# FFN columns on partitions between up and down, with block transposes around the quantization, and all clips on GpSimd from the fifth unit on

## The chip, the cores and the metric

The kernel runs on one core of a Trainium2 chip. Five of the core's parts matter here: TensorE (PE in the profile, with its weight loads as PEld), VectorE (DVE), ScalarE (ACT), GpSimd (POOL), and the queue of SyncE (SP), which issues nearly all transfers. The metric is the device time of one execution in microseconds. Before the change it is 3705.63 us, the median of three runs from 3700.53 to 3706.57.

## The reference

One transformer layer over x of 8 sequences by 1024 tokens by 512, all in float32: a layer norm, latent attention (16 heads, 32 content and 16 rotary dimensions a head, scores clipped to +-80, causal softmax), a residual, a second layer norm, a feed-forward network whose linear layers quantize both operands to FP4 in blocks of 16 along the contracted dimension, and a residual.

```python
def fp4_quant_dequant(x):                       # BLOCK = 16, along the last dim
    xb = x.reshape(shape[:-1] + (shape[-1] // BLOCK, BLOCK))
    scale = jnp.maximum(jnp.max(jnp.abs(xb), axis=-1, keepdims=True) / 6.0, 1e-12)
    xn = xb / scale
    idx = jnp.searchsorted(_MID, jnp.abs(xn))
    return (_GRID[idx] * jnp.sign(xn) * scale).reshape(shape)

gate = fp4_linear(x, w_gate)                    # w_gate, w_up: 1408 x 512
y = fp4_linear(x, w_up)
h = jax.nn.silu(gate) * y
return fp4_linear(h, w_down)                    # w_down: 512 x 1408
```

So the 1408 columns of h are quantized in blocks of 16 neighbours before the last product contracts over them.

## The kernel before

The 8192 tokens are cut into 16 units of 512 (two per sequence), each of 4 tiles of 128 tokens; the FFN has 64 tiles. The orders of PE, DVE and ACT are written out by the program: it runs its Python loops once and keeps, in `Clock`, an estimate of when each of the three engines will be free. DVE work that isn't urgent waits in two queues, `soon` (sums of the softmax, norms of x) and `later` (FFN norms and quantization). `on_dve` places an instruction that has a due time and first fills the estimated gap ahead of it from the queues; `need(key)` places all that is queued up to a key, just before PE uses that result. GpSimd's and SyncE's instructions stand in the order in which the program makes them.

*Attention* (`attention`, `score_step`). For each group of four heads, and each block of 128 keys, PE makes scores into one PSUM tile, ACT takes exponentials in two halves, each half is clipped (the first by DVE, L531, the second by GpSimd, L534), GpSimd masks both halves of the diagonal blocks (L538), DVE adds the weights up (L560; from the fifth unit on always, `FIRST = 4`), and PE multiplies them with the values one step later. The clip of the first half goes through `on_dve`, so it is also a point where queued DVE work is placed.

*Fillers.* Between the steps PE gets pieces of other work from a list, in proportion to cost: the next unit's projections, in the first four units the quantization and transposition of the weights (`weight_pieces`), and from the fifth unit on the FFN (`ffn_pieces`). After the last step of attention the rest of the FFN runs alone: some four and a half tiles.

*FFN per tile of 128 tokens.* Tokens lie on the partitions. `fetch` loads y from the memory where `out_proj` left it, `begin` queues its norm and its quantization, `turned` has PE transpose y in four blocks of 128x128 (`turn`, L184) and ACT copy them out. `gate` and `up` multiply with the transposed y as the stationary operand and the weights moving, in three pieces of 512, 512 and 384 columns (`FCH`); ACT copies gate out (L126), takes silu of all 1408 columns at once (L730), and DVE multiplies up into it (L742). `quantize` treats the 1408 columns as one: the maxima of its 88 blocks (L197), six small instructions for the scales (L202 to L207), then per piece a scaling (L224), two instructions for the step (L232, L235), an addition and a subtraction that round to it (L238), and the scaling back (L220). Then PE transposes h in 11 blocks (`hidden_turned`, three groups of 4, 4 and 3), ACT copies these out as hT (L186), and `down` contracts over 11 blocks, 512 columns wide. Between up and down of a tile lie down of the tile before and gate of the tile after.

Every fp32 matmul is two passes of PE in the profile, each with a weight load; the count of a group is that of passes.

*Norms.* `normed` has DVE take mean and variance (L302 to L304), GpSimd raise the variance to the power -0.5 (L305), and DVE apply both (L308). DVE's next instruction after L304 is mostly L308 itself.

Of the kernel before, what the change touches and what calls it, by code (L numbers as in the profile page):

```python
# [42 lines left out]
def tile_mla_then_fp4_ffn(  # L43
# [22 lines left out]
    p4 = ctx.enter_context(tc.tile_pool(name="p4", bufs=4))  # L66
    small = ctx.enter_context(tc.tile_pool(name="small", bufs=2))
# [121 lines left out]
    def quantize(q, width, key):  # L189
        nb = width // BLK  # L190
        q3 = q.rearrange("p (b k) -> p b k", k=BLK)
        got = {}

        def amax():
            got["sc"] = sc = p1.tile([P, 88], F32, tag="sc", name="sc")[:, :nb]
            got["rs"] = rs = p1.tile([P, 88], F32, tag="rs", name="rs")[:, :nb]
            nc.vector.tensor_reduce(rs, q3, AX.X, ALU.max, apply_absolute_value=True)  # L197
# [11 lines left out]
        slack(0.06 + 0.0011 * width, amax, key)  # L209
        slack(1.1 + 0.008 * nb, scales, key)  # L210
        for o in range(0, width, 512):
            step = min(512, width - o)
            part, bl = q[:, o : o + step], slice(o // BLK, (o + step) // BLK)
# [31 lines left out]
            slack(pass_cost, lambda f=times: f("sc"), key)  # L245


    def weight_pieces():
# [10 lines left out]
        def load(i):  # L259

            if i % 3 < 2:
                raw = p2.tile([P, FF], F32, tag="h", name="wraw")
            else:
                raw = p1.tile([P, NFC, P], F32, tag="hT", name="wraw_hT")
                raw = raw.rearrange("p n k -> p (n k)")
            raws[i], at = raw, 0
            for src, _ in chunks[i]:
                nc.sync.dma_start(out=raw[:, at : at + src.shape[1]], in_=src)
                at += src.shape[1]
            quantize(raw[:, :at], at, ("w", i))  # L270

        def piece(i, at, dst, off, n):
            if i == 0 and at == 0:
                for k in range(3):
                    load(k)
            clk.need(("w", i))
            turn(raws[i][:, at : at + n * P], dst[:, off : off + n], n)
            if at + n * P == sum(src.shape[1] for src, _ in chunks[i]):
                raws.pop(i)
                if i + 3 < len(chunks):  # L280
                    load(i + 3)

        pieces = []
        for i, parts in enumerate(chunks):
            at = 0
            for src, dst in parts:
                for off, width in FCH if src.shape[1] == FF else [(0, D)]:
                    n = width // P
                    pieces.append((i, at, dst, off // P if src.shape[1] == FF else 0, n))
                    at += width  # L290
# [33 lines left out]
    def project_pieces(u):  # L324
# [31 lines left out]
        def rotation(g):  # L356
# [15 lines left out]
            krp = p1.tile([P, 256], F32, tag="krp", name="krp")  # L372
# [103 lines left out]
    def score_step(u, hq, j, qc, qr, acc, aT):  # L476
# [48 lines left out]
        for k, (half, ready) in enumerate(zip(halves, done)):  # L525
            part = pT[:, half, :cols]
            if k == 0:
# [100 lines left out]
    def attention(u):  # L628
# [6 lines left out]
        total, gone = sum(c for c, _ in fillers), 0.0  # L635
        aTs = []
        for hq in range(NQ):
# [5 lines left out]
            for j in range(nj):  # L643
# [7 lines left out]
                while fillers and (gone + fillers[0][0] / 2) * whole < total * spent:  # L651
                    c, run = fillers.popleft()
# [11 lines left out]
    mids, outs = {}, {}  # L664
# [5 lines left out]
    def out_proj(u, t, aTs):  # L670
# [19 lines left out]
        mids[u, t] = mid  # L690
        if t == NT - 1:
            del live["wo"]


    tiles = [(u, t) for u in range(2 * B) for t in range(NT)]
    ys, hs, ends = {}, {}, {}
# [5 lines left out]
    def begin(n):  # L702
        begin_norms([(ys[n], ("y", n))])
        quantize(ys[n], D, ("y", n))

    def hidden(n, w, off, width):
        pg = bank("pg")[:, :width]
        for i in range(NDC):
            mm(
                pg,  # L710
                lhsT=ys[n][:, i, :],
                rhs=w[:, i, off : off + width],
                start=(i == 0),
                stop=(i == NDC - 1),
            )
        return pg

    def turned(n):
        clk.need(("y", n))
# [217 lines left out]
```

## Time and profile before

| | us |
|---|---|
| median of three runs | 3705.63 |
| the profiled execution | 3706.02 |
| its span, first to last instruction | 3704.3 |
| PE busy | 3611.4 |
| DVE busy | 2702.0 |
| ACT busy | 1279.7 |
| POOL busy | 660.9 |

Busy times are sums over the span; a wait is the idle time of an engine ahead of an instruction, put down to what ended it. Matmuls overlap in the pipeline, so a matmul's duration is longer than the distance to the next; what a row of matmuls costs is read from their starts. "xN" is a number of instructions.

### The profile page before, as it was taken

To read this page: it belongs to the slowest core of one execution; us is meant where nothing else is said; L and a number is where in the kernel's file an instruction comes from. 1 tells how busy PE (TensorE), PEld (TensorE's weight loads), DVE (VectorE), ACT (ScalarE), POOL (GpSimd) and SP (SyncE) were. 2 spreads that over 40 slices of the span, in tenths; PEclk is the share of its full clock that TensorE was granted. 3 is DMA by queue.
4 is the path that set the end of the run, shared out by engine and by line. 5 is a ranking of instruction groups with operands and counts; after the bars stand their busy time and mean duration, and the time that the engine had idled before them with its cause. 6 is when DMAs were issued, how large, how long until landed. Compare 5 with 4: busy or idle time off the path is not lost.

```text
span 3704.3 us, 45379 instructions
## 1 busy us (share of the span) xinstructions
PE 3611.4 (97%) x18052; PEld 1632.5 (44%) x18052; DVE 2702.0 (73%) x4775; ACT 1279.7 (35%) x1722; POOL 660.9 (18%) x838
## 2 busy tenths in 40 slices
PE   7898989999999999999999999999999999999999
PEld 3333334444444444444444444444444444444444
DVE  5866846777776787776777676878667787768875
ACT  3343443333323333333333233333233333333311
POOL 2223221111111111111111111111111111111200
PEclk9999999999999999999999999999999999999999
DMA  3101101010010100020100101000110001010010
GB/s 84 58 30 53 63 17 43 24 57 24 18 57 18 54 18 23 18 63 23 43 23 18 57 24 49 21 20 27 54 43 23 23 18 57 18 46 18 15 60 15
DMA packets 75884, 131.20 MB, mean 35 GB/s; under 512 B 13720, under 2 KB 14744, under 8 KB 75672
## 3 DMA queue, kind: packets, MB, share of 16 engines
q1 hardware_dynamic: 73824, 127.17, 10.9%
q8 instruction: 142, 2.33, 0.3%
q10 hardware_dynamic: 1848, 1.13, 0.1%
q14 instruction: 70, 0.57, 0.1%
HBM read 94.72 MB, written 33.55 MB: 35 GB/s over the span
## 4 chain that ended last, share of the span: by engine, by line
PE 83%; DVE 1%; ACT 1%; DMA 1%; POOL 0%; issue 0%; SPq 0%; ACTq 0%; POOLq 0%
PE pg L113 32%; PE pd L113 17%; PE sc_ps L113 11%; PE num L113 6%; PE po L113 5%; PE pt L184 3%; PE pp L113 2%; PE den L113 1%; PE pqr L113 1%; PE pk L113 1%; PE pv L113 1%; PE pq L113 1%; ACT pT L516 1%; DMA wo<-in_w_o_dram 0%; PE pf L113 0%
## 5 line engine op out<-in xcount | busy, mean ns | idle before, releaser
L516 ACT ACTIVATE pT<-sc_ps 128x1024 f32<-128x1024 f32 (+1 forms) x640 | 566.0, 936 | 1004.9 <-PE sc_ps L113 779.2
L113 PE MATMUL pg<-wu_T,yT 128*128 128x512 f32 (+1 forms) x1536 | 637.2, 562 | 6.9 <-ACT kT L126 5.1
L113 PE MATMUL pd<-wd_T,hT 128*128 128x512 f32 x1408 | 640.6, 596 | 0.0
L113 PE MATMUL pg<-wg_T,yT 128*128 128x512 f32 (+1 forms) x1536 | 632.7, 563 | 1.5 <-ACT yT L186 1.5
L534 POOL TENSOR_SCALAR pT<-pT 128x1024 f32<-128x1024 f32 (+1 forms) x320 | 336.4, 1051 | 1063.2 <-ACT pT L516 742.7
L538 POOL TENSOR_SCALAR_AFFINE_SELECT pT<-pT 128x256 f32<-128x256 f32 (+1 forms) x384 | 239.3, 623 | 1539.9 <-DVE pT L531 1228.7
L560 DVE TENSOR_TENSOR pT<-pT 128x1024 f32<-128x1024 f32 (+3 forms) x528 | 464.6, 904 | 8.0 <-POOL pT L538 4.6
L531 DVE TENSOR_SCALAR pT<-pT 128x1024 f32<-128x1024 f32 (+1 forms) x320 | 213.7, 668 | 342.8 <-ACT pT L516 341.8
L113 PEld LDWEIGHTS pg<-wg_T,yT 128*128 128x128 f32 x1536 | 287.7, 191 | 329.4 <-issue 259.5
L113 PEld LDWEIGHTS pg<-wu_T,yT 128*128 128x128 f32 x1536 | 281.7, 191 | 295.1 <-issue 231.2
L113 PEld LDWEIGHTS pd<-wd_T,hT 128*128 128x128 f32 x1408 | 255.4, 191 | 280.7 <-issue 270.5
L113 PE MATMUL sc_ps<-qc,kT 32*128 32x512 f32 (+3 forms) x3072 | 340.2, 527 | 4.3 <-ACT pT L516 4.2
L113 PE MATMUL num<-pT,v 128*32 128x512 f32 (+3 forms) x3072 | 321.8, 498 | 10.7 <-POOL pT L538 6.3
L742 DVE TENSOR_TENSOR h<-pg,h 128x512 f32<-128x512 f32 (+1 forms) x192 | 123.7, 644 | 279.2 <-PE pg L113 267.1
L113 PE MATMUL sc_ps<-qr,kr 32*128 32x512 f32 (+3 forms) x3072 | 306.5, 483 | 4.3 <-DVE qr L452 4.3
L126 ACT COPY h<-pg 128x512 f32<-128x512 f32 (+1 forms) x192 | 105.5, 550 | 544.4 <-PE pg L113 544.4
L238 DVE TENSOR_TENSOR h<-h,m 128x512 f32<-128x512 f32 (+1 forms) x384 | 261.1, 680 | 10.5
L113 PE MATMUL po<-wo,aT 128*128 128x512 f32 x512 | 224.7, 597 | 11.6 <-DMA wo<-in_w_o_dram 10.3
L186 ACT COPY hT<-pt 128x512 f32<-128x512 f32 (+1 forms) x192 | 105.4, 550 | 302.6 <-PE pt L184 302.0
L113 PEld LDWEIGHTS sc_ps<-qc,kT 32*128 32x128 f32 x3072 | 114.8, 184 | 200.7 <-issue 157.4
L113 PEld LDWEIGHTS sc_ps<-qr,kr 32*128 32x128 f32 x3072 | 145.6, 186 | 108.6 <-issue 82.4
L113 PEld LDWEIGHTS num<-pT,v 128*32 128x32 f32 x3072 | 67.0, 108 | 217.5 <-issue 142.4
(99 smaller groups left out, 3615.4 us busy)
## 6 DMA issues: line engine op xcount, KB each, us to landing
xo<-in_x_dram SPq DMA_DIRECT2D x64, 256.0 KB, 2.7
wo<-in_w_o_dram SPq DMA_DIRECT2D x16, 1024.0 KB, 5.4
mid<-xo SPq DMA_DIRECT2D x64, 256.0 KB, 2.3
y<-mid SPq DMA_DIRECT2D x64, 256.0 KB, 2.6
xr<-mid SPq DMA_DIRECT2D x64, 256.0 KB, 2.6
out_dram<-xr SPq DMA_DIRECT2D x64, 256.0 KB, 2.0
xl<-in_x_dram SPq DMA_DIRECT2D x62, 256.0 KB, 2.7
wraw<-in_w_gate_dram SPq DMA_DIRECT2D x8, 256.0 KB, 2.7
```

What stands on the lines that cost most here:

```text
L113: nc.tensor.matmul(dst, **kw)
L126: on_act(0.1 + 0.0009 * src.free_size(), lambda: nc.scalar.copy(dst, src))
L184: nc.tensor.transpose(pt[:, i, :], src[:, i * P : (i + 1) * P], ident)
L186: on_act(0.56, lambda: nc.scalar.copy(dst, pt[:, 0:n, :]))
L238: nc.vector.tensor_tensor(part, part, got["m"], op)
L516: lambda: nc.scalar.activation(part, sc[:, 2 * k : 2 * k + 2, :cols], AF.Exp, scale=SM_SCALE),
L531: lambda: nc.vector.tensor_scalar(part, part, E_HI, E_LO, ALU.min, ALU.max),
L534: nc.gpsimd.tensor_scalar(part, part, E_HI, E_LO, ALU.min, ALU.max)
L538: nc.gpsimd.affine_select(out=diag, in_=diag, pattern=[[0, 2], [0, len(segs)], [1, P]], compare_op=ALU.is_ge, fill=0.0, base=0, channel_mu ...
L560: lambda a=whole, b=part: nc.vector.tensor_tensor(a, a, b, ALU.add),
L742: lambda: nc.vector.tensor_tensor(h, pg, h, ALU.mult),
```

## The change

The FFN works on pairs of tiles (256 tokens). `turned` still transposes y per tile, into two halves of 256 tokens (`yTs`). `hidden` has the weights stationary and y moving: each of the 11 blocks of 128 columns of gate and up comes out with the columns on the partitions and 256 tokens along the free axis, two blocks to a PSUM tile, so six pieces of gate and six of up a pair. `down` takes h as it lies, as the stationary operand; `hidden_turned`, the tile hT and its copies are gone. Since 16 neighbouring columns now lie on 16 partitions, `quantize` with `turned=True` has DVE transpose each part in place in blocks of 32x32 before the maxima and again after the scaling back. h is quantized in three groups a pair (two pieces each; in the last pair the last two pieces are groups of their own), each queued as soon as its last up is through, and silu is taken after every second piece of gate. The order of a pair is gate 0, 1, up 0, 1, both downs of the pair before, gate 2, 3, up 2, 3, gate 4, 5, up 4, 5, with the loads and norms of the next pair between. The parts come from a pool `ring` of nine tiles of 512 columns, which the weights' loads use too.

From the fifth unit on (`u >= FIRST`) GpSimd clips both halves of a step. The rotary product of the keys (`krp`) is written into the place of its result. Pieces of the FFN carry their tile, and attention doesn't take a piece whose tile has not gone through `out_proj`.

```diff
+    ring = ctx.enter_context(tc.tile_pool(name="ring", bufs=9))
...
-    def quantize(q, width, key):
-        nb = width // BLK
-        q3 = q.rearrange("p (b k) -> p b k", k=BLK)
+    def quantize(parts, key, turned=False):
+        ends, at = [], 0
+        for part in parts:
+            ends.append((at, at + part.shape[1] // BLK))
+            at = ends[-1][1]
+        nb = at
...
+        def turn_blocks(part):
+            slack(
+                0.06 + 0.0013 * part.shape[1], lambda: nc.vector.transpose(part, part), key
+            )
...
-        slack(0.06 + 0.0011 * width, amax, key)
+        for k, part in enumerate(parts):
+            if turned:
+                turn_blocks(part)
+            slack(0.06 + 0.0012 * part.shape[1], lambda k=k: amax(k), key)
         slack(1.1 + 0.008 * nb, scales, key)
...
             slack(pass_cost, lambda f=times: f("sc"), key)
+            if turned:
+                turn_blocks(part)
...
-            if i % 3 < 2:
-                raw = p2.tile([P, FF], F32, tag="h", name="wraw")
...
+                for off in range(0, src.shape[1], 512):
+                    width = min(512, src.shape[1] - off)
+                    raw = ring.tile([P, 512], F32, tag="h", name="wraw")[:, :width]
+                    nc.sync.dma_start(out=raw, in_=src[:, off : off + width])
...
-            krp = p1.tile([P, 256], F32, tag="krp", name="krp")
+            krp = proj[u][2][:, g * 256 : (g + 1) * 256]
...
-            if k == 0:
+            if k == 0 and u < FIRST:
                 on_dve(
...
+                    if len(fillers[0]) > 2 and tiles[fillers[0][2]] not in projected:
+                        break
...
-        quantize(ys[n], D, ("y", n))
-    def hidden(n, w, off, width):
-        pg = bank("pg")[:, :width]
+        quantize([ys[n]], ("y", n))
+    def turned(n):
+        m, t = divmod(n, 2)
+        clk.need(("y", n))
+        if t == 0:
+            yTs[m] = [ring.tile([P, 2, 256], F32, tag="h", name="yT") for _ in range(2)]
+        pt = bank("pt").rearrange("p (n k) -> p n k", k=P)
         for i in range(NDC):
-            mm(
-                pg,
-                lhsT=ys[n][:, i, :],
-                rhs=w[:, i, off : off + width],
-                start=(i == 0),
-                stop=(i == NDC - 1),
-            )
+            nc.tensor.transpose(pt[:, i, :], ys[n][:, i * P : (i + 1) * P], ident)
+            clk.pe += 0.11
+        ys.pop(n)
+        for i in range(2):
+            to = yTs[m][i][:, :, t * P : (t + 1) * P]
+            on_act(0.38, lambda: nc.scalar.copy(to, pt[:, 2 * i : 2 * i + 2, :]))
+    def hidden(m, w, k):
+        n = min(2, NFC - 2 * k)
+        pg = bank("pg").rearrange("p (n k) -> p n k", k=256)[:, :n]
+        for c in range(n):
+            f0 = (2 * k + c) * P
+            for i in range(NDC):
+                mm(
+                    pg[:, c, :],
+                    lhsT=w[:, i, f0 : f0 + P],
+                    rhs=yTs[m][i // 2][:, i % 2, :],
+                    start=(c == 0 and i == 0),
+                    stop=(c == n - 1 and i == NDC - 1),
+                    skip_group_check=True,
+                )
         return pg
...
+        if k % 2 == 1:
+            def silu(hk=hs[m][k - 1 :]):
+                for h in hk:
+                    on_act(0.2 + 0.0009 * h.free_size(), lambda: nc.scalar.activation(h, h, AF.Silu))
+                clk.act += 2.6
+            silus.append(silu)
...
+        for group in ((0, 1), (2, 3), (4,), (5,)) if m == pairs - 1 else ((0, 1), (2, 3), (4, 5)):
+            if k == group[-1]:
+                quantize([flat(hs[m][j]) for j in group], ("h", m, k // 2), True)
...
-    def hidden_turned(n, k):
...
-        turn(hs[n][:, off : off + width], hTs[n][:, f0 : f0 + c, :], c)
...
     def down(n):
-        hT = hTs[n]
+        m, t = divmod(n, 2)
+        if t == 0:
+            fetch_x1(n + 1)
         pd = bank("pd")
-        for i in range(NFC):
-            mm(pd, lhsT=hT[:, i, :], rhs=wd_T[:, i, :], start=(i == 0), stop=(i == NFC - 1))
...
+        for c in range(NFC):
+            if t == 0 and c % 4 == 0:
+                clk.need(("h", m, c // 4))
+            mm(
+                pd,
+                lhsT=hs[m][c // 2][:, c % 2, t * P : (t + 1) * P],
+                rhs=wd_T[:, c, :],
+                start=(c == 0),
+                stop=(c == NFC - 1),
+            )
...
+            yield from run(gate, 0)
+            if m > 0:
+                yield 0.0, n, lambda m=m: fetch_x1(2 * m - 2)
+            if m < last:
+                yield 0.0, n + 2, lambda n=n: fetch(n + 1)
+                yield 0.0, n + 2, lambda n=n: fetch(n + 2)
+            yield from run(gate, 1)
+            if m < last:
+                yield 0.0, n + 2, lambda n=n: begin(n + 1)
+            yield from run(up, 0, 1)
+            if m > 0:
+                yield 9.6, n, lambda m=m: down(2 * m - 2)
+                yield 9.6, n, lambda m=m: down(2 * m - 1)
+            if m < last:
+                yield 0.0, n + 2, lambda n=n: begin(n + 2)
+            yield from run(gate, 2, 3)
+            yield from run(up, 2, 3)
+            yield from run(gate, 4, 5)
+            if m < last:
+                yield 0.5, n + 2, lambda n=n: turned(n + 1)
+            yield from run(up, 4)
+            if m < last:
+                yield 0.5, n + 2, lambda n=n: turned(n + 2)
+            yield from run(up, 5)
```

## The prediction

> **What bounds the kernel now.** I read the page first (shares, the span in 40 slices), then busy time by stretch, then who waits for whom, then groups by form, then stretches of the timeline for the spacing of instructions, which the groups' means don't give.
>
> ```profile
> PE 3611.4 (97%) x18052; PEld 1632.5 (44%) x18052; DVE 2702.0 (73%) x4775; ACT 1279.7 (35%) x1722; POOL 660.9 (18%) x838
> ...
> PE   7898989999999999999999999999999999999999
> ...
> DVE  5866846777776787776777676878667787768875
> ...
> PEclk9999999999999999999999999999999999999999
> ```
>
> PE is full from the seventh slice to the end, at the full clock. DVE, the next engine, is at six to eight tenths.
>
> ```profile
> 900.00:1200.00 300.00, 297.37 (x1427) 136.70 (x1426) 218.75 (x389) 104.08 (x141) 50.01 (x68) 1.00 0.10 32
> ...
> 3300.00:3600.00 300.00, 297.80 (x1302) 133.03 (x1301) 240.34 (x415) 94.45 (x119) 44.36 (x50) 1.00 0.09 29
> ```
>
> Columns: length, then busy PE, PEld, DVE, ACT, POOL, clock, DMA. Over 600 to 3650 us the stretches leave PE idle for 17.5 us in all; 69 us lie in the first 600 us and 6 in the last 54. So in the FFN part an instruction taken from PE is worth its spacing, as long as no other engine comes late.
>
> ```profile
> PE num L113 <- POOL pT L538: 6.3, 8, 1.6
> ...
> PE sc_ps L113 <- ACT pT L516: 4.2, 12, 0.8
> ...
> PE pt L184 <- DVE h L220: 2.5, 1, 2.5
> ```
>
> This is PE's list of waits (total, times, longest). For the quantized h it waited once in 64 tiles, at the very end. DVE's 73% has always come in time so far.
>
> **The change, part by part.** I sum against the profiled execution: 3706.0 us (span 3704.3 and 1.7 around it), 0.4 above the median of the three runs.
>
> *PE, removed: the transposes of h.*
>
> ```profile
> 3565.79 9.61 PE L113 MATMUL pg<-wg_T,yT 128*128 128x512 f32 x24
> 3575.24 0.60 PE L184 MATMUL pt<-ident,h 128*128 128x128 f32 x4
> 3575.68 3.60 PE L113 MATMUL pg<-wu_T,yT 128*128 128x512 f32 x8
> 3579.11 0.60 PE L184 MATMUL pt<-ident,h 128*128 128x128 f32 x4
> 3579.55 6.18 PE L113 MATMUL pg<-wu_T,yT 128*128 128x512 f32 x16
> 3585.57 3.60 PE L113 MATMUL pd<-wd_T,hT 128*128 128x512 f32 x8
> 3589.00 0.49 PE L184 MATMUL pt<-ident,h 128*128 128x128 f32 x3
> 3589.32 3.60 PE L113 MATMUL pd<-wd_T,hT 128*128 128x512 f32 x8
> ```
>
> Durations overlap, so the price is from start to start: 0.44, 0.44 and 0.32 us, 1.20 a tile, and 64 tiles give **-76.8 us**. All of it is on the path. The 8 transposes of y per pair stay.
>
> *PE, changed: gate and up.* Now a tile's gate takes 24 passes (two per fp32 matmul) in 3575.24 - 3565.79 = 9.45 us, and up 3.43 + 6.02 = 9.45: 64 x 18.9 = 1209.6 us. Afterwards the weights are stationary and 256 tokens move: 2 x 1408 matmuls, 5632 passes of 256 columns, the same columns in 1.8 times as many instructions and weight loads. The latents have just that shape:
>
> ```profile
> 1629.20 1.89 PE L113 MATMUL pp<-xnT,wdq 128*128 128x256 f32 x8
> 1631.02 0.64 PE L113 MATMUL pf<-krp,fold_sb 128*32 128x256 f32 x8
> ```
>
> Eight passes in 1.82 us; 0.09 of it is the switch to a 32-row group behind them (16 passes of up take 6.02 us ahead of pd above, but 6.11 ahead of a score group, 1689.58 to 1695.69). So 0.216 us a pass, and 5632 x 0.216 = 1216.5: **+7 us**. The other end takes the 1.82 whole: 0.2275 a pass, +72. I take 0.216: the weight load of this form (row below) lasts 0.194 us and fits under it. down keeps its 704 matmuls of 512 columns.
>
> *DVE, added and removed.*
>
> ```profile
> L113 PEld LDWEIGHTS pp<-xnT,wdq 128*128 128x128 f32 x256 | 48.7, 194 | 22.7 <-issue 12.7 <-ACT kT L126 1.4 <-DVE y L238 0.8
> ...
> L620 DVE STREAM_TRANSPOSE rc<-one 128x512 f32<-128x512 f32 x64 | 45.4, 710 | 1.8
> ...
> L531 DVE TENSOR_SCALAR pT<-pT 128x1024 f32<-128x1024 f32 x192 | 142.3, 741 | 190.9 <-ACT pT L516 190.2
> ```
>
> Block transposes: 2 x 160 of 512 columns at 0.71 = 227 us, and 64 of 256 columns, between 0.36 (half) and 0.71, taken as 0.39 = 25. Maxima: 160 of 512 columns at 0.686 (the y form) and 32 of 256 at about 0.36 = 121, against 64 x 1.613 = 103: +18. Scales: 97 groups of at most 64 blocks, between the six y instructions' 1.39 us and the h ones' 2.09, interpolated 1.8 and 1.6: 167 against 133, +34. The five passes keep their columns. Clips that leave: 144 x 0.741 + 96 x 0.557 = -160. Together +144 us.
>
> *POOL* gets these 240 clips at 1.153 and 0.899 us (its own rows), +252: 661 to 913 us, a quarter of the span. What that does to DVE is not free:
>
> ```profile
> 1689.06 1.41 DVE L220 TENSOR_TENSOR y<-y,sc 128x512 f32<-128x512 f32 x1
> ```
>
> The same product takes 0.69 us when POOL is idle (3683.13 in the tail); here a POOL clip of 1.36 us ran (1688.57 to 1689.93). Each moved clip can cost DVE 0 to 0.72 us, 0 to 173 in all. I take 0.2, +48, because the forms' means lie only 3 to 14% over their undisturbed durations. DVE: 2702 + 144 + 48 = 2894 us, 79% of the new span.
>
> The Trainium skill has a harder rule ("SBUF — State Buffer", the bullets under the diagram of its sides): GpSimd and a VectorE instruction with two SBUF inputs share a port pair by an exclusive lock, and the second is blocked for the whole instruction. By it each clip could hold DVE for its whole length, 252 us, which would put DVE at 3098: 6 us more a pair, 92 where PE needs 94, so by the rule the sum would still be the same, but with no reserve left. The two rows just shown agree with blocking (1.41 is 0.69 and 0.72 of waiting); the means say that it is met seldom.
>
> *Waits on DVE.* DVE idles 342 us for the exponentials in front of its clips (by line); three quarters, 256 us, go. In exchange GpSimd's power for rstd (L305), which the norms wait for, stands behind both clips and masks of a whole step in the changed kernel's order of instructions, where now it usually stands between a mask and a clip. Now DVE waits 0.8 us each time (42.8 us, 53 times). A masked step is 2 x (1.15 + 0.56) = 3.4 us on POOL, and a step is due every 3049/240 = 12.7 us, so a wait is between 0.8 and about half a step, 6.3. I take 3, nearer the POOL time. In a pair's wall (3104 us from 600 on, less 55, over 32 pairs: 95.3) DVE then has 78 busy (2304 from 600 us on, + 192, over 32) and 2 y norms and 0.75 of an x pair at 3 = 8: 86 of 95.3, 90%. Now it is 72 busy + 9 of waits for ACT and POOL = 81 of 97, 84%. PE itself needs 94.1 (3104 less 24 idle and 70 saved, over 32). DVE's reserve shrinks from 16 to 10 hundredths. PE's 17.5 us of steady waits may grow accordingly; I take **+10 us**, with ends of -17 and the second rival below.
>
> *ACT* loses the hT copies (105 us) and gets 56 more table loads at 1.28 (+72), and the silus in 192 pieces. Cover: ACT is 35% busy and PE waits 4.2 us for exponentials in all. Without it a silu group would hold one score step by two loads and two pieces, about 3.7 us. *SP*: y for two tiles is fetched after the first gate of a pair, into slots that the last pair's transposes have freed; x1 for the residual one piece before it is used, 2.6 us to land. Behind these stand out_proj's xo and wo, which PE awaits 10.3 us already. Nothing taken, a few us either way. In the first four units only the loads' pieces differ: within 5 us.
>
> *The tail.* After the last up, DVE has to finish: it got the fifth and sixth columns' group only then. Between the third and last up lie 10.4 us of PE (12 + 12 matmuls at 0.432); 9.7 of them go to the group of 1024 columns, which takes 13.2 us at these prices, 3.5 are left, and the groups of 512 and 256 columns take 7.1 and 4.5: 15.1 us. PE has 8 matmuls of down to run (6.9 us), then idles 8.2. Now the last tile's wait is 2.5 + 0.6. **+5 us**.
>
> Sum: 3706.0 - 76.8 + 7 + 10 + 5 = 3651.
>
> **The rivals.** (1) *DVE's waits shrink*: without the clips DVE never stalls behind an exponential, and the steady waits of PE go. For it: that wait is DVE's longest. Against: its busy time rises by 192. 3706 - 77 + 7 + 5 - 17 = 3624. (2) *Slower: the wait for rstd takes the place of the wait for the exponentials.* If a norm waits half a step (6.3 us, 17 a pair) and DVE still has a quarter of its present waits for PE (15 a pair), a pair needs 78 + 17 + 4 = 99 us of DVE against PE's 94.1: 32 x 5 = 160 us late, 3706 - 65 + 160 = 3801. It decides the sign once DVE needs over 96.1 us a pair, 2 us more than PE (the gain of 65 over 32). For it: the POOL order. Against: stretches with 80% busy DVE leave PE 2 us idle in 300. A milder form, 0.5 to 1.9 us a pair, ends between 3667 and 3700. (3) *The 256-column passes don't hold 0.216 us in long rows*, since a load of 0.194 leaves 0.02 of room: at 0.2275, 3651 + 65 = 3716. Against: eight such passes in a row already take no more. (4) *The transposes were hidden anyway*: excluded by the starts above, which follow each other without a gap.
>
> **How the numbers follow.** My forecast 0.64, its own range 3632 to 3680. Rival 1 0.13. Rival 2 0.10, and its milder form 0.08. Rival 3 0.05. Up to 3700 the forecast and the milder form are in, rival 2 and 3 out (0.15); at the lower end half of rival 1 is in, so it lies at that case's 3624, with 4 below it for a shorter tail. So 3620 to 3700. Faster by over 0.2%, which is about 7 us and the least that a measurement of this kernel tells from nothing, in the forecast, rival 1 and the milder form: 0.85. Within: a share of rival 3, 0.03. Slower: 0.12.
>
> **What would show it.** No transposes of h, and gate and up at 256 columns 0.216 us from start to start; DVE near 2890 us; L531's wait for ACT left only in the first four units; idle in front of the norm's scaling (L308's counterpart) near 3 us each; one PE wait of about 8 us for h near the end. I am wrong if PE waits for h in most pairs, if DVE passes 3000 us, or if passes stand wider apart than 0.216.

## The result, and the profile after

The changed kernel takes 3670.41 us (median, 3667.24 to 3672.05) beside 3703.56 us for the kernel before in the same session: 0.9909 of it, with a 95% interval from 0.9892 to 0.9927. It is faster by 33 us, where 55 were forecast. The profiled executions are 3706.02 and 3672.05 us, their spans 3704.3 and 3670.3, so the spans differ by 34.0.

The page of the changed kernel: busy time, then tenths of busy time in 40 slices.

```profile
PE 3548.3 (97%) x19908; PEld 2048.6 (56%) x19908; DVE 2946.7 (80%) x5264; ACT 1266.3 (35%) x1778; POOL 901.8 (25%) x1078
...
PE   7999989999999999999999999999999999999998
...
DVE  5886857888878798867888688988678886788886
...
PEclk8999999999999999999999999999999999999999
```

PE still has 97% and looks full in every slice from the seventh on, as before. DVE went up by 245 us, POOL by 241. At this resolution nothing is wrong. Four of the stretches of 300 us show more (columns: length, then busy PE, PEld, DVE, ACT, POOL, clock, DMA share, GB/s):

```profile
900.00:1200.00 300.00, 292.16 (x1586) 174.97 (x1583) 243.98 (x438) 101.31 (x146) 77.64 (x94) 0.99 0.10 31
1200.00:1500.00 300.00, 299.97 (x1588) 180.71 (x1587) 255.24 (x442) 108.68 (x147) 71.79 (x80) 1.00 0.09 31
1500.00:1800.00 300.00, 292.19 (x1566) 170.50 (x1565) 237.83 (x436) 99.08 (x142) 76.77 (x94) 0.99 0.13 43
...
3000.00:3300.00 300.00, 288.82 (x1569) 165.14 (x1565) 228.75 (x414) 102.44 (x144) 77.38 (x93) 0.99 0.12 38
```

PE idles 7.84, 0.03, 7.81 and 11.18 us in them. Of these four, DVE has most to do from 1200 to 1500 (255 us), and there PE misses nothing (from 600 to 900, with 263 us of DVE, it misses 1.2); it loses time in stretches where DVE is less busy. So the loss does not look like a general shortage of DVE. It sits in a few places, which PE's list of waits names (total, times, longest):

```profile
PE pt L185 <- DVE xl L327: 36.0, 7, 6.4
PE po L114 <- DMA wo<-in_w_o_dram: 14.0, 4, 7.8
PE pt L741 <- DVE y L239: 14.0, 2, 7.2
...
PE pd L114 <- DVE h L213: 7.3, 3, 5.4
```

The first line was 17.6 us in 3 waits before. The four new ones stand at 1050, 1551, 2050 and 2551 us, each 4.68 us long: PE wants to transpose x of the next unit, and the norm hasn't been applied yet. Both engines around the first of these waits, PE and then DVE:

```profile
1050.20 1.08 PE L185 MATMUL pt<-ident,xl 128*128 128x128 f32 x4 [4.68 <-DVE xl L327]
1051.21 1.94 PE L114 MATMUL den<-pT,ones 128*32 128x512 f32 x8
```

```profile
1046.90 0.68 DVE L824 TENSOR_TENSOR xr<-pd,xr 128x512 f32<-128x512 f32 x1
1047.50 0.68 DVE L321 BATCH_NORM_STATS2 nx<-xl 128x6 f32<-128x512 f32 x1
...
1050.49 0.55 DVE L327 TENSOR_SCALAR xl<-xl,nx 128x512 f32<-128x512 f32 x1 [0.44 <-POOL nx L324]
```

PE ran out of work at 1045.5. DVE worked without a gap, but it reached the norm of x only at 1047.5, having done quantization of h before it. The eight passes of the denominators (den) span 1.94 us here; elsewhere, at 639.38, the same eight span 1.06. That is PE's clock, which shows in short stretches around the wait (columns as above):

```profile
1045.00:1050.00 5.00, 0.51 (x2) 0.00 (x0) 4.72 (x13) 0.00 (x0) 0.88 (x2) 0.99 0.14 52
1050.00:1053.00 3.00, 2.80 (x12) 0.92 (x12) 0.60 (x2) 0.58 (x1) 0.46 (x1) 0.50 0.51 114
1053.00:1058.00 5.00, 5.00 (x50) 2.66 (x47) 4.54 (x7) 1.51 (x2) 2.10 (x3) 0.97 0.33 87
```

After the wait the granted clock is 0.50 for 3.4 us, then full again.

A ledger of PE, worked out from the starts of its instructions in both traces (the distance to the next start goes to a group, idle time taken out; the last line is half of the length of all stretches with the clock at 0.50, outside PE's idle time, and is a part of the first three):

| | before | after | difference | forecast |
|---|---|---|---|---|
| transposes of h | 81.4 | 0 | -81.4 | -76.8 |
| gate and up | 1237.0 | 1241.7 | +4.7 | +7 |
| all other work of PE | 2293.0 | 2306.5 | +13.5 | 0 |
| PE idle, first 600 us | 69.0 | 62.1 | -6.9 | 0 |
| PE idle, from there to the last 60 us | 17.5 | 48.9 | +31.4 | +10 |
| PE idle, last 60 us | 2.5 | 7.3 | +4.8 | +5 |
| of the work: lost to the half clock | 23.3 | 31.2 | +7.9 | not there |

The differences of the first six lines add to the 34.0 of the spans, but for rounding. The forecast missed by 21 us: 21.4 more of waits in the middle and 13.5 more of other work, less what came out better, 4.6 at the transposes, 2.3 at gate and up and 6.9 at the start. Of the 13.5 us of other work, 10.9 are passes at half clock, most of them in the products behind a wait (po 6.3, pp 4.0).

### The profile page after: what moved, and what is told of

It is laid out like the page before. It is cut to its first block, busy times and chain, and to the rows that moved or that the text cites. A ratio compares the mean times of both kernels' runs of the same rounds, so it can differ in the third digit from the quotient of the medians.

```text
span 3670.3 us, 49871 instructions
## 1 busy us (share of the span) xinstructions
PE 3548.3 (97%) x19908; PEld 2048.6 (56%) x19908; DVE 2946.7 (80%) x5264; ACT 1266.3 (35%) x1778; POOL 901.8 (25%) x1078
## 3 DMA queue, kind: packets, MB, share of 16 engines
q1 hardware_dynamic: 74976, 127.17, 10.9%
q8 instruction: 157, 2.57, 0.3%
## 4 chain that ended last, share of the span: by engine, by line
PE 66%; DVE 17%; issue 2%; ACT 1%; POOL 1%; DMA 0%; POOLq 0%; DVEq 0%; SPq 0%
PE pg L114 27%; PE pd L114 11%; PE sc_ps L114 9%; PE po L114 5%; PE num L114 5%; DVE pT L580 3%; PE pp L114 2%; DVE h L257 2%; DVE h L213 1%; PE den L114 1%; DVE rs L203 1%; DVE m L251 1%; DVE h L243 1%; DVE m L254 1%; DVE h L239 1%
## 5 line engine op out<-in xcount | busy, mean ns | idle before, releaser
L554 POOL TENSOR_SCALAR pT<-pT 128x1024 f32<-128x1024 f32 (+1 forms) x560 | 593.3, 1059 | 1656.0 <-ACT pT L536 1468.2
L114 PE MATMUL pg<-yT,wu_T 128*128 128x256 f32 x2816 | 640.3, 381 | 1.6 <-ACT kT L127 1.6
L114 PE MATMUL pg<-yT,wg_T 128*128 128x256 f32 x2816 | 637.7, 382 | 1.5 <-DVE h L794 1.4
L114 PE MATMUL pd<-wd_T,h 128*128 128x512 f32 x1408 | 620.1, 596 | 7.3 <-DVE h L213 7.3
L114 PEld LDWEIGHTS pg<-yT,wg_T 128*128 128x128 f32 x2816 | 530.7, 190 | 125.8 <-issue 28.0
L114 PEld LDWEIGHTS pg<-yT,wu_T 128*128 128x128 f32 x2816 | 526.1, 190 | 118.6 <-issue 43.3
L114 PEld LDWEIGHTS pd<-wd_T,h 128*128 128x128 f32 x1408 | 264.6, 190 | 343.3 <-issue 316.6
L114 PE MATMUL sc_ps<-qc,kT 32*128 32x512 f32 (+3 forms) x3072 | 341.8, 530 | 5.4 <-ACT pT L536 5.3
L127 ACT COPY h<-pg 128x512 f32<-128x512 f32 x192 | 105.6, 550 | 698.9 <-PE pg L114 698.9
L794 DVE TENSOR_TENSOR h<-pg,h 128x512 f32<-128x512 f32 x192 | 122.7, 640 | 234.6 <-PE pg L114 234.2
L213 DVE STREAM_TRANSPOSE h<-h 128x512 f32<-128x512 f32 (+1 forms) x384 | 251.8, 660 | 5.4
```

What stands on the lines that cost most here:

```text
L114: nc.tensor.matmul(dst, **kw)
L127: on_act(0.1 + 0.0009 * src.free_size(), lambda: nc.scalar.copy(dst, src))
L213: 0.06 + 0.0013 * part.shape[1], lambda: nc.vector.transpose(part, part), key
L554: nc.gpsimd.tensor_scalar(part, part, E_HI, E_LO, ALU.min, ALU.max)
L794: lambda: nc.vector.tensor_tensor(h, pg, h, ALU.mult),
```

## The experiments

All runs are of whole kernels, each beside the kernel before on the same chip; in these sessions the kernel before has medians from 3703.6 to 3706.3 us, so a difference of 2 or 3 us between two sessions means little. Two theories stood at the start. By the first, DVE's total load delays PE, so whatever unloads DVE helps in proportion. By the second, DVE has time enough, and the written-out order places a few pieces of its work too close ahead of the PE instruction that needs them. In the written-out order of the changed kernel, the norms of the next unit's first two x tiles fall, by the program's own estimate, at the same moment as their transposes in units 8, 10, 12 and 14 (counted from one); in the kernel before, 13 to 17 us lay between.

**Clip undone.** The change without its part on clips: DVE takes the first half's clip again in all units.

```diff
-            if k == 0 and u < FIRST:
+            if k == 0:
```

> The changed kernel with VectorE clipping the first half of every step again, so the FFN part of the change alone. Removing the transposes (-77 us) doesn't depend on the clip. Theory A (the new waits of PE sit at a few places in the written-out order; VectorE's load is otherwise hidden): VectorE back up by some 160 us less the contention that goes, 3050 us busy, wait for exponentials ahead of the clip again 300 us or more, and the time within 10 us of the changed kernel's 3670, either way. Theory B (VectorE's load makes PE late): VectorE is then over 83% of the span and PE waits longer: 3690 or more.

Measured: 3661.33 us (3660.61 to 3661.84), 0.9886 [0.9871, 0.9900]. With more to do on DVE, the kernel is faster by 9 us, within the first expectation (though DVE waits for exponentials 224 us, not 300). Its page:

```profile
PE 3544.7 (97%) x19908; PEld 2047.7 (56%) x19908; DVE 3009.1 (82%) x5504; ACT 1265.9 (35%) x1778; POOL 675.4 (18%) x838
```

DVE is at 3009.1 us, 62.4 above the changed kernel, though the 240 clips alone account for 157.0 (209.8 us in L551's groups here, 52.8 in the changed kernel). So moving them to GpSimd had made DVE's other instructions 95 us longer: 0.39 us a clip. PE's order of instructions is the same in both traces. The four x waits stay, 4.28 us each; the six waits for the rotary product of the queries (`qr`, 4.3 us in the changed kernel) are gone.

**Clip alone.** The kernel before with nothing but the moved clips.

```diff
-            if k == 0:
+            if k == 0 and u < FIRST:
```

> The kernel before with only the clip part of the change: GpSimd clips both halves from the fifth unit on. PE's work is untouched and it idles 18 us in the steady part, so both theories expect 3704 within 7 us. VectorE busy falls by 160 less the contention: theory B's price of contention (0.43 us a moved clip, from 103 us of VectorE durations above their undisturbed values in the changed kernel) gives 2702 - 160 + 100 = 2640; the prediction's 0.2 gives 2590. If the power for rstd, which now stands behind whole steps on GpSimd, delays the norms, the wait of the norm's scaling rises from 0.8 us each to 3; if VectorE is late anyway, it stays under 1.

Measured: 3708.72 us beside 3704.14, 1.0012 [1.0003, 1.0021]: a loss of 4.6 us. DVE falls from 2702.0 to 2651.9, by 50 where clips of 162 left, so 112 us came back, 0.46 a clip. Waiting for the exponentials (80.9 us at L531) and for rstd, the result of GpSimd's power (34.8 us in 50), is short, as in the changed kernel.

**Norm earlier.** The piece that queues the norms of the next unit's first two tiles gets a higher cost, which by the merging of the lists brings the pieces behind it later and so gives the norm time.

```diff
-            (1.5, lambda: both(lambda: norms(0, 1), lambda: u > 0 or norms(2, 3))),
+            (4.0, lambda: both(lambda: norms(0, 1), lambda: u > 0 or norms(2, 3))),
```

> The changed kernel with one number altered: the piece that queues the norms of the first two x tiles counts 4.0 instead of 1.5 when pieces are merged, so that FFN pieces come between it and the transposes that need it. Theory A: the four waits of 4.68 us for the scaled x go (-19), perhaps with the 0.9 and 1.0 us waits that follow each of them (-8 more): 3651, between 3643 and 3655. Theory B: VectorE is late in any order, the waits move elsewhere: 3665 or more.

Measured: 3660.62 us (3659.66 to 3663.61), 0.9886 [0.9869, 0.9902], 10 below the changed kernel and between the two expectations. PE's waits in this run:

```profile
PE po L114 <- DMA wo<-in_w_o_dram: 19.8, 5, 8.1
PE pg L114 <- DVE h L794: 17.8, 7, 3.4
...
PE pt L185 <- DVE xl L327: 10.2, 3, 6.3
```

The four x waits are gone (18.7 us), and 7 us of those at the start. But the edit shifts PE's order too: in four places (3.37 us each) up now waits for a PSUM bank, a piece of PE's output memory, that the product (L794) has still to free, and the waits for wo grow by 6 us. The second theory explains the gain; that the gain is small is this exchange.

**No block transposes.** DVE's 384 in-place transposes are left out, so h is quantized along the wrong axis; the time tells what DVE's load is worth.

```diff
         def turn_blocks(part):
-            slack(
-                0.06 + 0.0013 * part.shape[1], lambda: nc.vector.transpose(part, part), key
-            )
+            pass
```

> The changed kernel without VectorE's block transposes (what is left out: blocks of 16 are then formed over tokens instead of columns). VectorE loses 252 us: 2947 to about 2690, less than before the change. Theory A: only the tail's wait (7.3 us, to 2 or 3) and a few small ones go: 3660 within 7. Theory B: PE's steady waits fall back to the 18 us of before, 3630 or less.

Measured: 3655.46 us (3652.69 to 3657.09), 0.9869 [0.9854, 0.9884]. Its page and PE's waits:

```profile
PE 3545.9 (97%) x19908; PEld 2047.8 (56%) x19908; DVE 2721.2 (74%) x4880; ACT 1266.3 (35%) x1778; POOL 899.8 (25%) x1078
```

```profile
PE pt L185 <- DVE xl L325: 34.8, 7, 6.2
...
PE pd L114 <- DVE h L237: 3.9, 2, 2.2
```

DVE has 225 us less to do, about what it had before the change, and the kernel gains 15, within the first expectation; 3.4 of them are waits at the end. PE's order is the same as in the changed kernel. The x waits are 34.8 us instead of 36.0, the four new ones 4.42 each, and PE idles 41.7 us in the middle instead of 48.9. This run decides against the first theory: a queue that is short of time would have given much of the 225 back.

**Fill point kept.** The clip on DVE was also a place where the program fills in queued DVE work. Here GpSimd clips, but the filling stays.

```diff
             else:
+                if k == 0:
+                    clk.fill(ready)
                 nc.gpsimd.tensor_scalar(part, part, E_HI, E_LO, ALU.min, ALU.max)
```

> The changed kernel, clips on GpSimd, but the planner fills VectorE's estimated gap at the place where the first clip stood (one call of fill with the same due time). The clip undone gave 3661. Theory F (the clip's call was also a point where queued VectorE work was placed, and without it norms and sums are placed late): 3661, within 3. Theory C (contention: GpSimd's clips lengthen VectorE's instructions, 110 of the 160 us come back, and they do so where PE waits): no gain, 3670 within 4.

Measured: 3670.69 us, 0.9906 [0.9891, 0.9921], the changed kernel's time. The lost places for filling don't explain what the moved clips cost.

**Clip undone and norm earlier together.** Each gained about 10 alone.

> The changed kernel with both edits that helped: VectorE clips the first halves again, and the norm's piece counts 4.0. If the two act at different places, their gains add: 3670.4 - 9.1 - 9.8 = 3651.5. If both only move the same lateness of VectorE at the same places: 3657 to 3661, and PE's wait for a PSUM bank behind VectorE (17.8 us with the norm earlier) stays.

Measured: 3679.46 us, 0.9930 [0.9913, 0.9947], slower than either and than the changed kernel; no expectation had this. PE's waits:

```profile
PE po L114 <- DMA wo<-in_w_o_dram: 29.3, 11, 8.0
PE pd L114 <- DVE h L213: 23.4, 19, 5.4
```

With DVE clipping, the shifted order leaves down without its h in 19 places. The two edits act on the same order, and their effects can't be added.

**Tail interleaved.** On top of the clip undone, the last pair's two downs take turns: blocks 0 to 3 of both tiles, 4 to 7 of both, then 8 to 10, so that PE has 16 matmuls instead of 8 that need nothing of the last group.

```diff
-        for t in range(2):
-            yield 9.6, 2 * pairs - 1, lambda t=t: down(2 * last + t)
+        yield 19.2, 2 * pairs - 1, lambda: down_both(last)
...
+        pds = [bank("pd") for _ in range(2)]
+        for cs in (range(0, 4), range(4, 8), range(8, NFC)):
+            clk.need(("h", m, cs[0] // 4))
+            for t in range(2):
+                for c in cs:
+                    mm(
+                        pds[t],
+                        lhsT=hs[m][c // 2][:, c % 2, t * P : (t + 1) * P],
...
```

> The clip undone, and the last pair's two downs run interleaved (contraction blocks 0 to 3 of both tiles, then 4 to 7, then 8 to 10), so that PE has 13.7 us of work instead of 6.9 while VectorE finishes the last two groups. If the wait at the end is VectorE's 15 us after the last up against PE's 6.9, as the prediction has it: the 7.2 us of waiting fall to 1 or less, PE's slow clock behind them goes too (up to 5 us), and the time is 3650 to 3654. If something else holds the end (the last group's own length, or the transfer out), it moves by 3 us or less, 3658 or more.

Measured: 3652.91 us (3651.38 to 3655.13), 0.9858 [0.9843, 0.9872], 8.4 below the clip undone and inside the first expectation. The end of PE's timeline in the changed kernel, then in this one:

```profile
3637.63 5.31 PE L114 MATMUL pd<-wd_T,h 128*128 128x512 f32 x12
3643.42 1.98 PE L114 MATMUL pd<-wd_T,h 128*128 128x512 f32 x4 [0.48 <-DVE h L213]
3650.80 3.71 PE L114 MATMUL pd<-wd_T,h 128*128 128x512 f32 x4 [5.40 <-DVE h L213]
3655.89 10.57 PE L114 MATMUL pd<-wd_T,h 128*128 128x512 f32 x24 [1.38 <-DVE h L213]
```

```profile
3622.35 15.61 PE L114 MATMUL pd<-wd_T,h 128*128 128x512 f32 x36
3640.61 5.40 PE L114 MATMUL pd<-wd_T,h 128*128 128x512 f32 x8 [2.65 <-DVE h L213]
```

The tail's waits fall from 7.3 to 2.65 us (the clip undone has 7.2). Of the half clock around them (in the changed kernel four passes take 3.71 us behind the 5.40 us wait, 1.98 at full clock) one stretch of 3.41 us is left: the eight passes behind the wait take 5.40 us, 3.60 at full clock. The clip undone has 10.24 us of it there. Waits and half clock at the end make 6.6 of the 8.4 us; the rest lies elsewhere. One of the waits remained, which I had expected at 1 us or less.

**No block transposes and norm earlier.** The same leaving out as above, with the norm's cost at 4.0.

> The changed kernel without VectorE's block transposes (left out, so blocks of 16 are formed over tokens) and with the norm's piece counting 4.0. It tells why the norm edit gave 10 us instead of the 20 that its four waits and the slow clock behind them cost. Theory O (order alone): the edit itself displaces something, and it gives 10 here too: 3655.5 - 10 = 3645.5. Theory L (load: with 2947 us VectorE has no reserve at these places, so the wait moves on to PE's wait for a PSUM bank, 17.8 us): with 252 us less on VectorE that wait shrinks to under 5 us, and the edit gives 18 or more: 3637 or less.

Measured: 3655.07 us, 0.9867 [0.9852, 0.9881], so the norm edit gives nothing here. The x waits are down to 9.9 us, but waits for the product of up (10.0 in 9), for the residual sum (8.0 in 4) and for the clipped and masked weights (10.7 in 20) stand in their place, and those for wo grow from 13.5 to 21.2 us. Neither expectation was met, and I don't know why these exchange so exactly.

**Norm earlier, tail interleaved.** The norm edit with the tail, clips on GpSimd as in the change.

> The changed kernel, GpSimd's clips kept, with the norm's piece at 4.0 and the interleaved end. The two act 600 us or more apart, so the gains should add: 3660.6 - 8.4 = 3652, within 3; if the end's gain depended on VectorE clipping, which it can't since no attention is left there, 3658 or more.

Measured: 3655.84 us, 0.9869 [0.9854, 0.9884], 4.8 below the norm edit alone, where 8.4 were expected; it lies between the two expectations. PE's last wait for h falls from 7.2 to 2.6 us, and its other waits are nearly as they were.

**FFN held back.** PE's longest single wait, 7.8 us at 3039 us in the changed kernel, is for the weights wo, at a unit's end where no FFN piece may be taken ahead of out_proj. Here, on top of the clip undone and the tail, unit 14 leaves 25 us of FFN to later units.

```diff
             budget = within * (13, 5)[u % 2 == 0] / left
+            if u == 13:
+                budget -= 25.0
```

> The kernel of the interleaved end (VectorE clips, 3652.9) with 25 us of FFN pieces moved from the fourteenth to the fifteenth unit. There the order has no FFN piece ahead of out_proj, since the next pair's tiles have not gone through out_proj yet, and PE waits 6.9 us for wo with its slow clock behind (6.83 us at half, 3.4 lost). If the missing pieces are the cause: that wait falls under 2 us and the time to 3643 to 3647. If wo comes late by itself (its buffer is one of the softmax's, which VectorE frees): the wait stays and the time too, 3650 or more.

Measured: 3676.59 us, 0.9923 [0.9907, 0.9940], 24 slower than without it. PE's waits:

```profile
PE pt L741 <- DVE y L239: 25.6, 6, 7.2
PE pd L114 <- DVE h L213: 13.9, 6, 5.7
...
PE po L114 <- DMA wo<-in_w_o_dram: 8.5, 5, 2.5
```

The long wait for wo went, as meant, and waits for y (4.3 and 6.6 us) and h (5.7 and 2.4) arose from 3330 us on. PE's waits of the middle grow from 41.9 to 56.7 us, and more stretches of half clock follow them. Where the held-back work is done, DVE is late.

**Norm earlier with PE's order kept.** The piece's cost is taken from the one ahead of it (2.5 together, as before), so that the norms are queued about 16 us earlier and PE's order stays nearly what it was; with the clip undone and the tail.

```diff
-            (1.0, lambda: fetch(0, 1)),
-            (1.5, lambda: both(lambda: norms(0, 1), lambda: u > 0 or norms(2, 3))),
+            (0.2, lambda: fetch(0, 1)),
+            (2.3, lambda: both(lambda: norms(0, 1), lambda: u > 0 or norms(2, 3))),
```

> The kernel of the interleaved end (VectorE clips, 3652.9) with the norms of the first two x tiles queued 16 us earlier by the plan, and nothing else of PE's order moved (the piece before counts 0.2 instead of 1.0 and the norm's piece 2.3 instead of 1.5, so that all later pieces stay where they were). It parts what the earlier norm edit mixed: a later norm's wait, and a displaced order. If the four waits of 4.28 us for x come from the norms being queued only when they are needed, they go with what follows them (0.87 and 1.1 us four times, and the slow clock, some 1.7 us four times): 3652.9 less 17 to 30, 3623 to 3636. If VectorE has no room for them earlier, PE waits for quantized h instead, as it did with the clip undone and the norm's piece at 4.0 (23 us in 19 waits): 3645 or more.

Measured: 3644.75 us (3644.28 to 3645.46), 0.9839 [0.9822, 0.9855]: 8 below the same kernel without it, though 17 to 30 were expected; it lies at the edge of the second expectation, and the sign of that one came. PE's waits:

```profile
PE pt L741 <- DVE y L239: 17.9, 3, 7.2
PE pt L185 <- DVE xl L327: 17.2, 3, 6.4
...
PE pd L114 <- DVE h L213: 10.5, 10, 2.6
```

The four x waits are gone (17.2 us, the three of the start, are left), but PE now waits for h ahead of down ten times instead of once, and for y once more. What DVE does earlier for x it does later for h and y.

**The same, clips on GpSimd as in the change.** So this is the changed kernel with the earlier norms and the interleaved tail.

> The best kernel so far (norms 16 us earlier, interleaved end, 3644.8) with the clips of the first halves on GpSimd again, as the change has them. Contention theory: they relieve VectorE by only some 60 us busy and lengthen its instructions where PE waits, so the loss of 9 us between the changed kernel and the one with the clip undone shows again: 3651 to 3656. Theory L (VectorE has too little room for the earlier norms: the waits for y and h that came, 4.3 and 10.5 us, shrink when VectorE clips less): 3641 or less.

Measured: 3634.41 us (3633.75 to 3635.78) beside 3704.98, 0.9809 [0.9793, 0.9825]. The second expectation (3641 or less) is met. It is the fastest kernel of this study, 36 us below the changed kernel. PE's waits and its timeline at the place that was shown at 1050:

```profile
PE pt L185 <- DVE xl L327: 17.2, 3, 6.4
PE pt L741 <- DVE y L239: 14.0, 2, 7.2
...
PE pd L114 <- DVE h L213: 2.7, 1, 2.7
```

```profile
1029.48 9.60 PE L114 MATMUL pd<-wd_T,h 128*128 128x512 f32 x22
1038.92 0.60 PE L185 MATMUL pt<-ident,xl 128*128 128x128 f32 x4
```

Without a mark of idle time ahead of it, the transpose follows down at once. Of the four x waits none is there, and of those for h only the one at the end, with DVE at 2941.3 us, as busy as in the changed kernel. PE's idle time in the middle is 30.5 us instead of 48.9, and the half clock costs 21.2 us of work instead of 31.2. The kernel before idled 17.5 us there; of the 13 us between, one wait for wo makes 8.

Beside the run before it, the moved clips now gain 10 us; in the change's own order they lose 9, and alone on the kernel before 4.6. The part of the change that is about clips has no sign of its own: it frees DVE of 157 us or a little more, makes 95 to 112 of it come back, and what remains counts only where an instruction of DVE is late. That fits the gain here, where waits for h go from 10.5 to 2.7 us and for y from 17.9 to 14.0, in the same order of PE. It does not explain the loss of 9 in the change's order. There, undoing it takes 8.1 us off PE's idle time: 4.3 at the waits for qr, 1.6 at the four x waits, the rest in small pieces. The waits for qr come with the moved clips here too (4.3 us in 6, none without), but there are waits for h and y to gain. Why DVE comes late to qr with them no run singles out.

## Why the prediction was right or wrong

**Direction and place of the gain: right.** The transposes of h were fully on the path: 81.4 us by the ledger, 76.8 forecast (0.4 of the difference is half clock; the rest are distances to the next start that are longer than the three in the tail). That excludes the rival by which they were hidden.

**Gate and up at 256 columns: right.** 16 passes of up lie between these starts in the changed kernel:

```profile
629.13 3.62 PE L114 MATMUL pg<-yT,wu_T 128*128 128x256 f32 x16
632.58 0.60 PE L741 MATMUL pt<-ident,y 128*128 128x128 f32 x4
```

That is 3.45 us, 0.216 a pass, as taken; +4.7 against +7, and +7.3 without the passes at half clock. The third rival (0.2275) is out.

**The tail: right.** One chain of waits of 0.48, 5.40 and 1.38, 7.3 us in all, against 8.2 worked out.

**PE's steady waits, "+10 us": this is the step that failed.** It let the 17.5 us of waits grow because "DVE's reserve shrinks from 16 to 10 hundredths". The waits grew by 31 us, and for the most part not by that reserve: 41.7 of the 48.9 us are left with 225 us less on DVE and 41.4 with 62 us more, and with DVE as busy as in the change but its norms queued earlier (and the end interleaved), 30.5 are left and the four x waits, 18.7 us, are gone. Of the other 13, the 7.8 us for wo at 3039 went only in the run that kept FFN pieces back for that place, which lost more elsewhere. What failed is the kind of argument. A mean over a pair tells whether DVE can keep up; it can't tell how long before its use one piece is queued. The order of pieces was there to be read: the changed list puts the norms of x at the moment of their transposes in four units. I had priced no place of this order. That 3670 still lies in the forecast's own range of 3632 to 3680 it owes to the width of the range: the term had the right sign, a third of the size, and a reason that the runs don't bear out.

**The half clock: a term that was missing.** A wait of PE was counted at its own length. From 600 us on, the half clock behind waits costs 13.8 us of PE's work where it cost 3.4 before; over the whole run it adds 7.9. The kernel before had it too, in a row that I passed over:

```profile
1561.47 5.40 PE L113 MATMUL pg<-wu_T,yT 128*128 128x512 f32 x8 [2.57 <-ACT kT L126]
```

Eight such passes took 3.60 us in the prediction's own rows, so 1.8 us followed the 2.57 of waiting.

**DVE's busy time: 2947 against 2894.** The block transposes are right (0.71 and 0.39 taken):

```profile
L213 DVE STREAM_TRANSPOSE h<-h 128x512 f32<-128x512 f32 x320 | 223.9, 704 | 4.5
...
L213 DVE STREAM_TRANSPOSE h<-h 128x256 f32<-128x256 f32 x64 | 28.1, 439 | 1.0
```

The mis-sized term is the contention, "I take 0.2, +48": 2946.7 less 2702 less the 144 of added and removed work leaves 101 us, 0.42 a clip, between the 0.39 and 0.46 of the two runs on clips. The reason given, that the forms' means lie close to their undisturbed durations, came from a kernel in which POOL was busy 661 us, and was used for 240 clips more. As a sum of DVE's time it counted for little, as the run without transposes shows. But the moved clips as a whole cost 9 us in the change's order (3661 us with the clip undone, against the 3651 forecast), for which the sum has no term.

**Waits for rstd, 3 us each: wrong.**

```profile
DVE pT L551 <- ACT pT L536: 76.8, 44, 5.7
...
DVE y L327 <- POOL ny L324: 35.3, 52, 0.7
```

DVE waits 0.7 us each time, less than before. POOL in turn waited for DVE ahead of rstd (589 us over 64 times, once a norm of y), so it was there first, and no clip stood in the way. With that, the second rival (slower by a wait for rstd) is out, the milder form too, although a time of 3670 lies inside the milder form's 3667 to 3700: right time, other cause. The upper line shows that waits for exponentials are left in the first four units only, as forecast: 341.8 us of them became 76.8.

**The first rival**, that PE's waits shrink, is out as well: it would need the opposite of what the middle did.

## What to carry to other kernels

Where the order is written out by the program, a change of the list of pieces moves every other piece: read, for each result that the bounding engine needs, how long before its use it is queued, and don't reason from the other engine's mean load. A wait in an otherwise full PE can cost more than its length, and a few waits of 5 us in the same place of every second unit are as visible in the trace as they are invisible in the 40 slices: look for stretches that differ in idle time. Price a clip moved to GpSimd with what it makes VectorE lose, and try it again after the order is mended, since its sign changed with the order.

## What the runs showed of the hardware

*The clock after a wait.* All stretches at a granted clock of 0.50 in the changed kernel's trace after the first 600 us are 3.41 or 6.83 us long, one and two of the same unit. They stand at every wait of 4.68 us and at those of 5.40 and 7.83, but waits of 2.57 differ: at 1561 us of the kernel before it is followed by one, at 1058 it is not. Of four places in the changed kernel (1128, 1629, 2128, 2629) where a wait of 1.02 us follows one of 0.68, two have one as well:

```profile
1127.70 3.08 PE L114 MATMUL pp<-xnT,wdkv 128*128 128x256 f32 x8 [1.02 <-DVE h L794]
...
1628.68 1.99 PE L114 MATMUL pp<-xnT,wdkv 128*128 128x256 f32 x8 [1.02 <-DVE h L794]
```

So for a short wait its length doesn't decide; its place does. The stretches of one trace begin whole multiples of 3.413 us apart, to 0.01 us (1049.93, 1128.44 and 1551.69 in the changed kernel: 23 and 147 units), as if time were cut into cells of that length. Both waits at 1128 lie in one cell (1125.03 to 1128.44, 1.69 us idle), and the next cell is at half clock; at 1629 a border at 1626.79 cuts the first wait, 1.25 us fall into the cell behind it, and none follows. The 2.57 us at 1561 lie in one cell too, those at 1058 in two, as 0.90 and 1.67. In all fourteen traces, after the first 14 us, no cell at full clock with less than 1.69 us of idle PE is followed by one at half clock, and every one with more than 2.02 is; in between both occur. A stretch without a wait of its own costs about 1.7 us of PE's work, half of 3.41.

The Trainium skill ("TensorE: Matmul & The Clock Gate", Part 1) has the clock fall to half after an idle window of about 3.4 us and says that the window is free-running. The length of the unit and the fixed cells agree with that; that half a window of idle time is enough, 1.69 us ahead of 1128.44, is less than the page's rule asks for.

*GpSimd beside VectorE.* 240 clips of 1.1 and 1.0 us on GpSimd cost VectorE 95 to 112 us, 0.39 to 0.46 us each. The norm's scaling, which is issued right behind GpSimd's power, shows it most:

```profile
L327 DVE TENSOR_SCALAR y<-y,ny 128x512 f32<-128x512 f32 x64 | 59.7, 933 | 35.4 <-POOL ny L324 35.3
```

It was 574 ns in the mean before (560 with the clip undone) and is 933 now; single ones take from 537 to 1370 ns. The Trainium skill ("SBUF — State Buffer", the section on its two sides) makes the ports that the two engines share an exclusive lock for a whole instruction, where VectorE's instruction uses them. By it the clips could hold VectorE for 252 us; the runs show two fifths of it, so on average a clip holds VectorE for less than half of its length; which instructions it spares wasn't measured. The prediction's own example agrees with the lock only roughly: the product of 1.41 us ended 0.54 us after the clip beside it (1690.47 and 1689.93), less than the 0.69 it takes alone, so by these records, which are rough for GpSimd, it was not held to the clip's end.
